# Post-norm two-layer block on one core: another assignment of two groups to the linear attention's buffers, four more early idle products, other priorities

## The chip, the cores and the metric

The kernel runs on one core of one Trainium2 chip. The metric is device time in microseconds (us) of one execution, lower is better. The time before is 608.35 us, the median of three runs (604.67 to 611.22). One further execution was profiled; it took 606.87 us, and its profile spans 605.1 us from the first instruction to the last.

Engine names in the profile: PE is TensorE (products; PEld its weight loads), DVE VectorE, ACT ScalarE, POOL GpSimd, SP the engine that issues the DMAs. L984 is line 984 of the kernel.

## The reference

Two layers, each an attention and a feed-forward part, with a layer norm behind each of the four residual sums. Shapes: x is 2 x 1024 x 128, all float32.

```python
x = layernorm(x + L0_attn(x))   # 8 heads, softmax over 1024 keys, 16-wide q/k, 128-wide v summed over heads
x = layernorm(x + L0_ffn(x))    # 128 -> 512 gated by silu, 512 -> 512 gelu, 512 -> 512 gelu, 512 -> 128
x = layernorm(x + L1_attn(x))   # linear attention, 4 heads of 32: short convolutions, delta rule in chunks of 32
x = layernorm(x + L1_ffn(x))    # +-1 weights: 256 -> 512 relu, 512 -> 512 relu, 512 -> 128
```

The delta rule is the part that the change touches:

```python
T = inv(eye + tril(kbeta k^T, -1)); u = T @ v; w = T @ kbeta     # per chunk of 32
for each of the chunks, in order:                                # a state S per batch and head
    u_i = u_i - w_i @ S
    o_i = q_i @ S + tril(q_i k_i^T) @ u_i
    S   = S + k_i^T @ u_i
o = gate * o + (1 - gate) * (p0 * v + p1 * fir_short(v) + p2 * fir_long(v))
o = rmsnorm(o) * rms_w @ Wo
```

## The kernel before, in words

**Tiling.** The 2048 rows of x are handled as four groups of 512: (0,0), (0,1), (1,0), (1,1), that is batch and half, called here the first to the fourth group. In the first attention there are eight units of 2 heads; two units make one group. A unit has two passes: `pass1` computes scores (L904) and takes their row maxima (L906 on DVE, for the first unit L909 and L912); a small transpose and two DMAs put the negated maxima back as an extra row of the queries (L921, L923, L925); `pass2` computes scores again (L944), exponentiates (L946 on ACT) and multiplies with the values (L951). The feed-forward part `ffn0` (L984) follows a group's attention, then `l1_attn`, then `ffn1` (L1502, L1503). Most wide products use a rounded part and a remainder of the activations, so that each weight is used with two products of 128x512.

**The linear attention** of one group goes through these steps: `l1prep` (transposes L802, convolutions as four products each, L1138), `l1gate` (L1187), `l1gram` (64 products of 32x32 tiles, L1087), `l1inv` (the triangular inverse, 30 small DVE operations at L1248 and L1249), `l1v` (values), `l1fir` (the long filter: 128 small products L1310, with Toeplitz blocks loaded by DMA into two small buffers `nm` and `pr`, or into a pool of five buffers of their own for the second and fourth group), `l1T`, `l1wu`, `l1scan` (16 dependent steps), `l1out`, `l1rms` (norm, product with Wo at L1494, layer norm). The group (1,1) needs the state of (1,0), and (0,1) that of (0,0).

It has two forms. The *early* form (`late` false) does the inverse first, and the filter after the scan; a scan step is four 32x32 products (L1087), the outputs are added in one accumulator (L1418, then L1474), and much of the elementwise work is on POOL. The *late* form does the filter ahead of the inverse; a scan step is one 128x128 product (L1451) with a block-diagonal operand that ACT has written before (`spread`, L1443: 16 copies a group), and elementwise work is on DVE and ACT.

**Buffers.** Three sets of buffers hold a linear attention at work: LA, allocated at the start, and two more, b and c, that take the place of the first attention's buffers when that has ended. `PLAN` says which set serves which groups in turn, `EARLY` for how many of a set's first jobs the early form is used. So before, LA serves the first group (early form) and later the fourth (late form), b the second and c the third.

**Order.** The program is recorded in full, then ordered by a planner in the kernel: a list scheduler with a price per instruction. An instruction's rank is its place in a backward plan minus 1000 times the entry of `AHEAD` for its step and group. `RUN` has two further settings: `switch`, a penalty in rank for changing the tile mode on PE, and `target`, the amount of recent PE work below which the planner puts an idle product (L1654, a product of constants that nobody reads) where it finds PE without work. So the order on each engine is fixed in the program, and the engines run it in order.

**Start.** PE begins with `KW` idle products on constants (L1555). Meanwhile SP loads x and the weights. Eleven weight blocks (`raw`, L726; two buffers) are rounded by ACT (L729), the remainder is taken by POOL (L731), and the pair goes back to DRAM (L732). x is normed, transposed (L802), copied by ACT (L831), and projected for the first unit (L681, evicted by ACT at L691 and L687 and by DVE at L692 and L688); the first group's other projections follow (L845, L846, L847).

Of the kernel before, what the change touches and what calls it, by code (L numbers as in the profile page):

```python
# [14 lines left out]
AX = mybir.AxisListType  # L15

MARK = HOOK = None
RUN = {'dummies': True, 'target': 3733.1600, 'rewarm': False, 'switch': 48514.8000}
TURNS = 5
AHEAD = {  # L20
    "ffn0": {"00": 114.739, "01": 79.0168, "10": 93.113, "11": 16.0},
    "ffn0b": {"00": 28.2844, "01": 46.0158, "10": 3.8711, "11": -177.442},
    "ffn0c": {"00": 7.2297, "01": 25.7048, "10": -2.4362, "11": -60.4919},
    "ffn1": {"00": -191.539, "01": -121.481, "10": -24.0187, "11": 13.6298},
    "ffn1b": {"00": -284.165, "01": -22.3296, "10": -26.57, "11": -37.1254},
    "ffn1c": {"00": -256.6, "01": -72.7131, "10": -43.7013, "11": -63.3199},
    "l1T": {"00": 58.5553, "01": 22.3564, "10": -115.222, "11": -15.058},
    "l1fir": {"00": 17.0418, "01": -65.313, "10": -9.4956, "11": -94.8684},
    "l1gate": {"00": 17.4596, "01": 74.4737, "10": -71.5563, "11": -51.9871},
    "l1gram": {"00": 71.0216, "01": 57.0343, "10": -34.4912, "11": -131.985},  # L30
    "l1inv": {"00": 101.529, "01": 187.238, "10": 97.6443, "11": -28.7276},
    "l1out": {"00": 8.2038, "01": 36.0016, "10": -49.0412, "11": -16.0023},
    "l1prep": {"00": 54.5467, "01": 18.6949, "10": -147.8, "11": -271.429},
    "l1rms": {"00": 19.507, "01": -139.242, "10": 56.2064, "11": -6.9188},
    "l1scan": {"00": 163.921, "01": -154.275, "10": -73.3537, "11": 123.217},
    "l1v": {"00": -45.706, "01": -14.4063, "10": -35.6576, "11": -265.782},
    "l1wu": {"00": 79.4419, "01": -19.5293, "10": -135.414, "11": -46.8271},
    "norm_in": {"0": 132.526, "1": 94.3253},
    "pass1": {"0": -45.1577, "1": -30.2813, "2": -37.2483, "3": 95.0868, "4": 22.2969, "5": -1.3221, "6": 36.2671, "7": 34.121},
    "pass2": {"0": -76.6421, "1": -27.8145, "2": 96.4425, "3": 23.5257, "4": 37.498, "5": 101.764, "6": 71.2041, "7": 34.7045},  # L40
    "post": {"00": 115.214, "01": 91.5204, "10": 25.9715, "11": 449.774},
    "prep": {"": 90.1269},
    "stacks": {"00": 12.9701, "01": -34.2909, "10": 54.0568, "11": 10.2821},
    "stk": {"0": -41.2247, "1": -35.7513, "2": 76.077, "3": 65.1726, "4": -27.8862, "5": 37.4738, "6": -56.9189, "7": 103.575},
    "warm": {"": 115.175},
    "weights": {"": 146.31},
}
HALVES, RU = 1, 1
KW = 40
ZLO, CVG, XH, TR, FE = 0, 1, 1, 5, 1  # L50
O1, O2, O3, O4 = 0, 1, 1, 1
LEND = (4, 2)
# [2 lines left out]
NI = 26  # L55
TB = 4
FA0 = 1
EARLY = {"fa": 2, "la": 1}
BANKS = (1, 2, 1, 1)
XJ = {"0": 3, "l": 1, "1": 3}  # L60
PLAN = [
    [("0", 0), ("0", 1), ("0", 2), ("0", 3), ("1", 0), ("1", 1), ("1", 2), ("1", 3)],
    [("l", 0), ("l", 3)],
    [("l", 1)],
    [("l", 2)],
]
GROUPS = [(0, 0), (0, 1), (1, 0), (1, 1)]

# [466 lines left out]
def body(ctx: ExitStack, tc: tile.TileContext, A, out, dbg=None):  # L535
# [6 lines left out]
    def mark(label):  # L542
        plan.marks.append((len(nc.cur_bb.bb.instructions), label))
        if MARK:
            MARK(nc, label)
# [1003 lines left out]
    def front():  # L1549
# [3 lines left out]
        wp = psv.tile([128, 512], F32, tag="pv", name="wp")  # L1553
        for n in range(KW):
            nc.tensor.matmul(wp, rest[:, 0:128], rest, start=True, stop=True)  # L1555
# [45 lines left out]
    def jobs(bufs, todo, extra=None):  # L1601
        for n, (kind, gi) in enumerate(todo):
# [3 lines left out]
            while need not in ready or (kind == "l" and GROUPS[gi][1] and ("l", GROUPS.index((GROUPS[gi][0], 0))) not in ready):  # L1606
                yield None
            yield from {"0": ffn0, "l": l1_attn, "1": ffn1}[kind](bufs, gi, n >= EARLY.get(bufs.nm, 0))
            if kind in "0l":
# [36 lines left out]

    plan.run(rank, least=WARM, **RUN)
    mark("idle")
# [109 lines left out]
```

## Time and profile before

| what | value |
|---|---|
| median of three runs | 608.35 us (604.67 to 611.22) |
| profiled execution | 606.87 us, of it 605.1 us span |
| mean granted TensorE clock | 0.988 |
| products of the first attention's last unit end (L951) | 355.6 us into the span |
| last product of the whole program (L1066) | 597.4 us |
| exponentials, L946 on ACT | 131.4 us and 12.1 us, 603 and 605 ns each |
| row maxima, L906 on DVE | 141.2 us, 681 ns each |
| loads of ACT's function tables | 17, 1283 ns each |

The shares of busy time are means over stages. From about 45 us to about 560 us PE is busy nearly all the time; ahead of that it shares the lead with loads and evictions, and behind it a chain of dependent steps sets the end. Two things are to be kept in mind for PE. A float32 product shows as two matmul records and two weight loads (64 products at L1474 show as 128 records), a rounded or bfloat16 one as one of each. And a stretch marked "issue" is one in which PE waited for nothing that the profile shows.

### The profile page before, as it was taken

How to read it: one execution, taken by the hardware profiler on the slowest of the kernel's cores; microseconds unless marked ns; L12 is line 12 of the kernel's file. 1: busy time of each engine (PE TensorE's matmuls, PEld its weight loads, DVE VectorE, ACT ScalarE, POOL GpSimd, SP SyncE). 2: the span in 40 equal slices, each digit the busy share in tenths (PEclk: the TensorE clock that was granted, in tenths of full speed). 3: DMA queues.
4: the chain of work that ended last, by engine and by line, in shares of the span. 5: the costliest groups of instructions: out<-in, count | busy, mean ns of one | idle time of the engine just before them, and what ended most of it. 6: DMA issues, size and time to landing. Idle time of an engine off the chain costs nothing.

```text
span 605.1 us, 17727 instructions
## 1 busy us (share of the span) xinstructions
PE 568.6 (94%) x7496; PEld 360.5 (60%) x7496; DVE 402.2 (66%) x975; ACT 340.5 (56%) x619; POOL 232.2 (38%) x317
## 2 busy tenths in 40 slices
PE   8789999999999999999999999999999998899984
PEld 4255455557675656556656466756777576677753
DVE  4758787786645798488974212397654967777763
ACT  3656467765768776865858564444434543434331
POOL 8845017212300726030397024437562361623210
PEclk9979999999999999999999999999989999999998
DMA  8886330025221306203121045315343013102220
GB/s 280 295 296 220 77 87 2 2 53 163 98 71 70 86 14 180 70 1 106 54 73 43 31 144 181 105 28 170 110 158 121 4 38 101 40 22 78 98 72 17
DMA packets 26737, 58.39 MB, mean 96 GB/s; under 512 B 4065, under 2 KB 12897, under 8 KB 26658
## 3 DMA queue, kind: packets, MB, share of 16 engines
q1 hardware_dynamic: 26658, 57.26, 30.2%
q8 instruction: 59, 0.97, 0.7%
q14 instruction: 20, 0.16, 0.1%
HBM read 41.19 MB, written 8.39 MB: 82 GB/s over the span
## 4 chain that ended last, share of the span: by engine, by line
PE 78%; DMA 7%; ACT 5%; DVE 4%; issue 2%; POOL 2%; SPq 1%; POOLq 0%; DVEq 0%; ACTq 0%
PE ps L984 19%; PE pv L951 10%; PE s L944 10%; PE ps L904 9%; PE ps L1087 7%; PE ps L1138 5%; PE ps L1503 4%; PE ps L1502 4%; DMA raw<-wf 2%; PE ps L1451 2%; PE ps L1310 2%; DMA x<-x 1%; DMA q<-mr 1%; DMA nm<-toep 1%; ACT p L946 1%
## 5 line engine op out<-in xcount | busy, mean ns | idle before, releaser
L906 DVE TENSOR_REDUCE mp<-ps 128x1 f32<-128x512 f32 x224 | 141.2, 681 | 52.0 <-PE ps L904 51.3
L946 ACT ACTIVATE p<-s 128x512 f32<-128x512 f32 x236 | 131.4, 603 | 49.4 <-PE s L944 40.8
L984 PE MATMUL ps<-ahi,w 128*128 128x512 f32 x352 | 123.1, 420 | 1.2 <-ACT u L1038 0.8
L944 PE MATMUL s<-q,k 128*128 128x512 f32 x236 | 92.1, 423 | 2.5 <-DMA q<-mr 1.6
L904 PE MATMUL ps<-k,q 128*128 128x512 f32 x240 | 85.2, 419 | 2.7 <-DVE m L912 1.4
L984 PEld LDWEIGHTS ps<-ahi,w 128*128 128x128 f32 x352 | 64.5, 190 | 28.4 <-issue 6.1
L951 PE MATMUL pv<-p,va 128*32 128x512 f32 x512 | 72.6, 601 | 0.0
L984 PE MATMUL ps<-alo,w 128*128 128x512 f32 x176 | 70.0, 400 | 0.2 <-POOL alo L998 0.2
L944 PEld LDWEIGHTS s<-q,k 128*128 128x128 f32 x236 | 42.3, 188 | 33.3 <-ACT p L946 16.8
L904 PEld LDWEIGHTS ps<-k,q 128*128 128x128 f32 x240 | 43.9, 190 | 26.5 <-DVE mp L906 10.2
L1502 PE MATMUL ps<-ahi,w 128*128 128x512 f32 x96 | 40.6, 423 | 3.2 <-DVE alo L1518 2.3
L1503 PE MATMUL ps<-alo,w 128*128 128x512 f32 x96 | 39.4, 412 | 1.1 <-DVE alo L1518 0.7
L1517 ACT ACTIVATE ahi<-ps 128x512 fp32r<-128x512 f32 x32 | 18.5, 597 | 37.5 <-PE ps L1503 37.4
L984 PEld LDWEIGHTS ps<-alo,w 128*128 128x128 f32 x176 | 33.5, 190 | 8.8 <-issue 0.7
L1138 PE MATMUL ps<-xT,wc 128*128 128x512 f32 x72 | 35.9, 609 | 0.8 <-POOL xT L1125 0.8
L1020 POOL TENSOR_TENSOR alo<-u,ahi 128x512 fp32r<-128x512 f32 x16 | 20.5, 1282 | 38.9 <-ACT ahi L1019 38.8
L1518 DVE SCALAR_TENSOR_TENSOR alo<-ps,ahi 128x512 fp32r<-128x512 f32 x32 | 21.4, 685 | 13.5 <-ACT ahi L1517 13.2
L786 POOL TENSOR_SCALAR r<-mv 128x4 f32<-128x4 f32 (+1 forms) x24 | 6.3, 265 | 60.9 <-DVE mv L784 55.5
L951 PEld LDWEIGHTS pv<-p,va 128*32 128x32 f32 x512 | 13.1, 108 | 26.6 <-issue 24.6
L1038 ACT ACTIVATE u<-ps,small 128x512 f32<-128x512 f32 x16 | 11.0, 687 | 26.9 <-PE ps L984 26.7
L976 POOL TENSOR_TENSOR y<-y,x 128x256 f32<-128x256 f32 x8 | 6.3, 788 | 51.4 <-DVE y L975 51.4
L1454 DVE TENSOR_TENSOR tt<-ps,an 128x32 f32<-128x32 f32 x64 | 11.9, 186 | 20.9 <-PE ps L1087 12.5
(274 smaller groups left out, 1034.9 us busy)
## 6 DMA issues: line engine op xcount, KB each, us to landing
w<-wd SPq DMA_DIRECT2D x56, 512.0 KB
wd<-w SPq DMA_DIRECT2D x14, 512.0 KB
raw<-wf SPq DMA_DIRECT2D x11, 256.0 KB
pj<-vC SPq DMA_DIRECT2D x32, 64.0 KB
toep<-toep SPq DMA_DIRECT2D x16, 128.0 KB
q<-hi SPq DMA_DIRECT2D x14, 128.0 KB
k<-hi SPq DMA_DIRECT2D x28, 64.0 KB
xt<-x SPq DMA_DIRECT2D x4, 256.0 KB
```

The lines of the kernel that those rows point to most:

```text
L904: nc.tensor.matmul(p, q[:, s * 128:(s + 1) * 128], d, start=True, stop=True)
L906: nc.vector.tensor_reduce(mp[:, s, e, i:i + 1], p, AX.X, ALU.max)
L944: nc.tensor.matmul(s2, ks[e][:, t * 128:(t + 1) * 128], q[:, i * 512:(i + 1) * 512], start=True, stop=True)
L946: nc.scalar.activation(p, s2, AF.Exp, scale=0.25)
L951: together([nc.tensor.matmul(pv[32 * j:32 * j + 32, :], va[:, t - 1, 2 * pr + j % 2, :], pend[j % len(pend)], start=(t == 1), stop=(t == 8 ...
L984: nc.tensor.matmul(p, w(k), a(k), start=(k == 0 and n == 0), stop=(k == nk - 1 and n == len(pr) - 1))
L1020: nc.gpsimd.tensor_tensor(lo[:, m, :], u, hi[:, m, :].bitcast(F32), ALU.subtract)
L1087: r.append(nc.tensor.matmul(p(hs), lhsT(hs), rhs(hs), start=True, stop=True, tile_position=(32 * h, 32 * h)))
L1138: nc.tensor.matmul(p, wc[:, w, t, :], xTh[:, t:t + 512], start=t == 0, stop=t == 3)
L1502: nc.tensor.matmul(p, w(k), ahi(k), start=(k == 0), stop=False)
L1503: nc.tensor.matmul(p, w(k), alo(k), start=False, stop=(k == nk - 1))
L1518: nc.vector.scalar_tensor_tensor(lo, p, 0.0, hi.bitcast(F32), ALU.max, ALU.subtract)
```

## The change

Three settings are changed, and the priorities with them; no function is edited.

```diff
-RUN = {'dummies': True, 'target': 3733.1600, 'rewarm': False, 'switch': 48514.8000}
+RUN = {'dummies': True, 'target': 4397.5100, 'rewarm': False, 'switch': 72754.5000}
...
-    "l1out": {"00": 8.2038, "01": 36.0016, "10": -49.0412, "11": -16.0023},
-    "l1prep": {"00": 54.5467, "01": 18.6949, "10": -147.8, "11": -271.429},
+    "l1out": {"00": 43.059, "01": 90.2521, "10": -47.2495, "11": 1.5469},
+    "l1prep": {"00": 44.7584, "01": -7.3587, "10": -133.55, "11": -298.276},
...
-    "weights": {"": 146.31},
+    "weights": {"": 109.692},
 }
...
-KW = 40
+KW = 44
...
-EARLY = {"fa": 2, "la": 1}
+EARLY = {"fa": 2, "la": 2}
...
 PLAN = [
     [("0", 0), ("0", 1), ("0", 2), ("0", 3), ("1", 0), ("1", 1), ("1", 2), ("1", 3)],
-    [("l", 0), ("l", 3)],
+    [("l", 0), ("l", 2)],
     [("l", 1)],
-    [("l", 2)],
+    [("l", 3)],
 ]
```

All 27 rows of `AHEAD` have other numbers. LA now serves the first and the third group, both in the early form, and the set c the fourth group, in the late form.

Counted in the two built programs, instructions that differ in number (from -> to):

| engine | instructions |
|---|---|
| PE | L1451 48 -> 32; L1474 64 -> 128; L1555 40 -> 44; L1654 35 -> 47 (in all 4470 -> 4534 products) |
| ACT | L1443 48 -> 32; L1259 12 -> 8; L1329 3 -> 2; table loads 17 -> 19 (one more at L946, one more at L1038) |
| DVE | L1334 6 -> 4; L796 on attention outputs 12 -> 8; L1288, L1344, L1347, L1430 3 -> 2 each |
| POOL | L1261 4 -> 8; L796 on attention outputs 20 -> 24; L1337 and L1338 2 -> 4 each; L1288, L1331, L1344, L1347 1 -> 2 each; L1368 6 -> 4; L1431 3 -> 2 |
| SP | 251, the same DMAs in another order |

The order changes on all engines. The main moves on PE, by place among the products (0 is the first; first to last product of a step):

| step, group | before | after |
|---|---|---|
| idle products L1555 | 37 ahead of the first transposes, 3 behind | 44 ahead |
| last unit's `pass2` ends | 1719 of 4470 | 1703 of 4534 |
| `l1rms` first group | 2291-2294 | 2138-2141 |
| `l1prep` third group | 2136-2295 | 2143-2318 |
| `l1scan` second group | 3013-3555 | 2922-3267 |
| `l1scan` third group | 3557-4024 | 3212-3467 |
| `l1fir` third group | 2559-2871 | 3432-3773 |
| `l1prep` fourth group | 2769-3015 | 3162-3272 |
| `l1gram`, `l1T` fourth group | 3087-3198, 3632-3863 | 3343-3423, 3829-4006 |
| `l1wu`, `l1scan` fourth group | 3869-4148, 4155-4287 | 4011-4220, 4235-4349 |

On ACT, the third rounding L729 moves from behind the two copies L831 to ahead of them, and each later one stands one to four evictions further ahead than before.

## Prediction

> **What bounds the kernel now.** I read the page first, then busy time by stretches, the groups by line, the chain of waits, and the timeline of the start.
>
> ```profile
> PE 568.6 (94%) x7496; PEld 360.5 (60%) x7496; DVE 402.2 (66%) x975; ACT 340.5 (56%) x619; POOL 232.2 (38%) x317
> PEclk9979999999999999999999999999989999999998
> ```
>
> PE leads at 94%, and its clock is low in one slice only. Stretches (us; busy us and instructions of PE, PEld, DVE, ACT, POOL; clock; DMA):
>
> ```profile
> 40.00:44.00 4.00, 4.00 (x14) 3.02 (x14) 1.40 (x4) 2.50 (x5) 2.44 (x3) 0.50 1.03 371
> 475.00:495.00 20.00, 19.77 (x656) 13.48 (x659) 16.27 (x43) 10.85 (x24) 13.63 (x18) 1.00 0.09 29
> 495.00:515.00 20.00, 17.03 (x684) 13.75 (x674) 14.76 (x53) 8.03 (x21) 2.17 (x5) 1.00 0.28 78
> 515.00:535.00 20.00, 18.34 (x677) 13.88 (x677) 16.07 (x51) 7.03 (x19) 12.95 (x13) 1.00 0.09 30
> 583.00:605.00 22.00, 12.52 (x53) 8.75 (x52) 9.56 (x29) 5.12 (x9) 2.53 (x4) 0.90 0.08 25
> ```
>
> PE has 1 to 3 us of slack per 20 us late on, and a tail of dependent steps. Groups (count | busy us, mean ns | idle before):
>
> ```profile
> L1451 PE MATMUL ps<-tt,pj 128*128 128x32 f32 x96 | 17.1, 260 | 0.3 <-DVE tt L1454 0.3
> L1654 PE MATMUL ip<-rest 128*128 128x512 bf16 x35 | 9.9, 381 | 0.0
> L1474 PE MATMUL ps<-tt,kv 32*32 32x32 f32 x128 | 1.5, 194 | 0.0
> ```
>
> Chain of waits (start, us, what):
>
> ```profile
> 151.00 2.73 PE ps L984 x12
> ...
> 360.60 4.37 DMA nm<-toep
> ...
> 501.89 1.42 PE ps L1087 x84
> 503.31 0.34 PE ps L1451 x2
> ...
> 505.33 0.84 issue
> 506.17 0.92 PE ps L1418 x60
> ...
> 512.65 0.94 issue
> 513.60 0.94 PE ps L1087 x62
> ```
>
> From these rows I price PE's work as it follows back to back: a wide product 0.2275 us (2.73/12), a small L1087 product 0.032 (about two records of 0.016), a scan step L1451 0.356 (17.1/48), an idle product 0.22 (four took 0.88 in the chain), a float32 512-column product 0.86 (L1138: two records took 0.86), a filter product 0.024, a transpose 0.13. The control: between the fourth group's first product (463.4 us) and the last product of its `l1wu` (543.7), 1380 products at these prices are 79.8 us; the trace has 80.3. The prices carry; what they miss is the sum of waits.
>
> The start, on ACT:
>
> ```profile
> 13.32 1.07 ACT L831 COPY xhT<-ps 128x512 f32<-128x512 f32 x2 [2.78 <-PE ps L802]
> 17.65 0.62 ACT L729 CAST w<-raw 128x512 fp32r<-128x512 f32 x1 [3.25 <-DMA raw<-wf]
> 18.18 0.68 ACT L691 ACTIVATE q<-ps,bqk 96x512 fp32r<-96x512 f32 x1
> ```
>
> The first eviction L691 stands behind a weight block that lands at 17.65.
>
> **The change, part by part.** *Start.* Seven more idle products ahead of the transposes put them 7 x 0.27 = 1.9 us later; covered, because the third L729 now stands ahead of the copies L831. The bytes ahead of its block on SP's queue are the same, so the copies wait for 17.65 and end at 19.35. L691 then also waits for the fourth block, at 20.89 before, now behind one 512 KB write in place of two, about 1.5 us earlier: L691 at about 20.3, 2.1 us late. Each further block needs POOL's L731 two blocks before (0.62 + 1.28 us, then about 3 us of load), so L846 comes at about 29.0 (26.91 before). Then it shrinks: before, the fifth L909 waited for the eighth block at 32.80; now that block stands four evictions earlier and ahead of the 448 KB load of `ku`, which puts the fifth L909 at 33.4 (33.33 before). The ninth block then delays the next three by 2 us, the small copy L923 (37.37 before) by 1.3, `biasv` (41.23) by 0.4. L944 starts at 45.57 and PE is full from 48 us on: what is late there stays late. I take +0.8; bounds -1.0 (the 1.4 us of idle PE in 32 to 36 us refilled) and +2.5 (nothing recovered).
>
> In the rows, the clock was 0.65 in 36 to 40 us and 0.50 in 40 to 44, though after the first 3 us no idle time of PE ahead of it was over 1.2 us; a thin stretch was enough. So I keep the same loss, and the new gap of about 3.3 us before L681 (15.7 to 19.0) at most doubles eight products of 0.6 us, inside waits. [...]
>
> *PE's work.* 16 scan steps go, -5.7; 64 products at L1474 come, 64 x 0.023 = +1.5; 12 idle products, 12 x 0.22 = +2.6: -1.6. But PE also pauses at "issue": nine times between 497.4 and 528.1, every 3.8 us, 0.08 to 0.94 us each, in stretches of 32 to 35 products' records and as many loads per us. In instructions the change adds 64 x 4 + 12 x 2 - 16 x 4 = 216; at some 256 per 3.8 us that is +3.2 where small products stand close. The new ones of the third group stand partly there. Bounds -4.2 (idle products free) and +3.2; I take -1.0, near the busy rows. [...]
>
> *ACT.* 16 copies L1443 go (-4.7 us, off PE's path); two table loads come, 2 x 1.28, in the last unit's exponentials (one more alternation of gelu and exp). PE lost 0.65 us in 350 to 360 with two alternations. Bounds 0 and 2.6; I take +0.6. DVE loses ten instructions (some 6 us), POOL gains 13 (some 12 us, 38% busy now) in the third group's filter and inverse, whose result is wanted hundreds of products later: nothing, as long as the third group is not last.
>
> *Shared LA.* The third group's `l1prep` must follow the first group's `l1rms`. Its Wo product waits for the chain L1478 to L1491, which at the row's durations (0.7, 0.7, 0.6, 0.7, POOL 0.2 and 2.9, 0.7, 0.7 and handovers) needs 8.8 us; PE has 9.5 us of work between the two. Bounds 0 and 2; +0.3. Queued behind that wait on PE is everything.
>
> *Fourth group.* Its chain now starts at product 3162 and has 63.1 us of PE work to the end of `l1wu`, against 79.8. From the last `l1gram` product to the first `l1T` PE has 22.4 us (25.1 before; the trace took 25.8). In between lie 52 DVE operations, 20 us, four ACT operations of 0.6 and handovers: about 24. From `l1T` to `l1wu` 9.1 us of work are enough (the second group did it in 9.3). So PE waits about 2 us. Bounds 0 and 9 (below).
>
> *Scan and tail.* 16.4 us of work lie in the last scan, 18.9 before (17.7 in the trace); a step of 0.36 plus L1454 0.19 and two handovers is 0.85 at least (first group: 0.85), 13.6 in all. I take -1.0; bounds -2.5 and 0. What follows, 34.4 us, is the same chain.
>
> Sum: 0.8 - 1.0 + 0.6 + 0.3 + 2.0 - 1.0 = +1.7 on 606.87, 608.6. The median of the runs lies 1.5 above that execution; between 608.6 and 610.1 I put 609.0.
>
> **The rivals.** *Slower: the fourth group's chain binds.* If `l1prep`-`l1gram`, `l1gram`-`l1T` and `l1wu`-`l1scan` keep the times that they had (20.6, 25.8, 15.2) where PE now has 17.9, 22.4 and 11.8 us of work, PE waits 2.7 + 3.4 + 3.4 = 9.5 us: 609.0 - 2.0 + 9.5 = 616.5. It decides from about 6 us of wait. For it: the compressed start; against: in the trace those times equal PE's own work, so the chain may be shorter.
>
> *Faster: the late pauses go.* The fourth group's stretch holds 4048 PE instructions in place of 5354 and 19 idle products as before; if the pauses (4.5 us in 497 to 528) and 2.5 us of idle in 495 to 535 fall away there, and the idle products fall only into waits (-2.6), 609.0 - 9.6 = 599.4. Against it: 5336 instructions in place of 3694 now stand between the attention's end and that point, and bring pauses of their own.
>
> *The changed order does nothing where it counts*: PE's work by the prices is equal to within 2 us, so only start and tables count, +1.4: 609.8 with the median's offset. It is inside the forecast's size class.
>
> **How the numbers follow.** Forecast (with the third rival) 0.44, slower rival 0.30, faster rival 0.26. A change of 1%, 6 us, is about what a measurement of this kernel can tell from none. The range reaches to both rivals' values: 599.4 to 617. The chances of faster, same and slower are these three.
>
> **What would show it.** In the changed profile: ACT's third L729 at about 17.6 with L831 behind it, L846 near 29; L944 starting by 46; the fourth group's first transpose near 480, and "issue" pauses more frequent ahead of it; idle on PE ahead of its `l1T` of 1 to 3 us (over 5: the slower rival; none, and few pauses: the faster); L1451 32 products. I am wrong on the whole if the last unit's L951 ends more than 5 us from 359.

## The result, and the profile after

The changed kernel takes 614.75 us (median of 16 runs, 610.18 to 618.74), the kernel before 608.72 in the runs beside them (16 runs, 604.67 to 612.90): ratio 1.011, 95% interval 1.0086 to 1.0135. It is slower by about 1%. Ratios, and the means in the table of the experiments, leave out runs over 1.5% above the fastest of the same kernel; medians hold all runs. The profiled execution took 612.65 us, 610.9 of it span, 5.8 more than before.

The busy line and the granted clock of the page:

```profile
PE 573.1 (94%) x7608; PEld 361.8 (59%) x7608; DVE 396.3 (65%) x965; ACT 335.3 (55%) x600; POOL 243.3 (40%) x330
PEclk9879999999999999999999999899999999899998
```

Two slices of the start are low now in place of one, and two behind the attention (not counting the last). Stretches (us; busy us and instructions of PE, PEld, DVE, ACT, POOL; clock; DMA share, GB/s):

```profile
20.00:24.00 4.00, 4.00 (x6) 1.45 (x7) 2.48 (x3) 2.00 (x4) 4.00 (x4) 0.57 0.81 228
40.00:44.00 4.00, 4.00 (x10) 2.46 (x11) 1.40 (x4) 2.61 (x6) 3.38 (x4) 0.50 0.83 253
44.00:48.00 4.00, 4.00 (x20) 3.64 (x19) 2.14 (x6) 1.19 (x2) 3.91 (x4) 0.58 0.59 237
392.00:396.00 4.00, 3.79 (x79) 2.90 (x79) 2.70 (x8) 0.59 (x1) 1.49 (x2) 0.57 0.01 4
475.00:495.00 20.00, 18.96 (x421) 11.86 (x410) 9.81 (x32) 7.60 (x18) 1.79 (x6) 1.00 0.01 3
495.00:515.00 20.00, 19.00 (x609) 12.17 (x605) 13.09 (x36) 5.51 (x10) 10.71 (x18) 1.00 0.15 48
515.00:535.00 20.00, 17.45 (x639) 12.14 (x632) 15.48 (x53) 4.66 (x8) 5.73 (x6) 0.91 0.35 101
583.00:605.00 22.00, 16.90 (x72) 11.04 (x71) 12.39 (x39) 6.74 (x11) 2.53 (x4) 1.00 0.11 36
```

Two of these stretches before:

```profile
20.00:24.00 4.00, 2.95 (x7) 0.78 (x6) 2.99 (x5) 2.88 (x5) 3.44 (x5) 1.00 0.75 205
44.00:48.00 4.00, 3.76 (x21) 2.73 (x20) 3.09 (x9) 2.59 (x6) 4.00 (x4) 0.99 0.27 105
```

Read the clock column. Taken in steps of 1 us it is 1.00, or falls to 0.50 in stretches of about 3.4 us, each of which loses 1.7 us of full clock. The profile of before has them at 37-44 (two, one behind the other) and at 446-451, that of after at 20-24, 37-48 (three), 392-396, 470-474 and 525-529: seven in place of three. (Each has some 2 us more at its very end, where PE has nothing left to do.)

Against this the milestones of the two profiles are: first L944 45.6 and 48.8 us, last L951 355.6 in both, end 605.1 and 610.9. So the start costs 3.2 us, the attention behind it is 3.2 us shorter, and the part behind the attention is 5.7 us longer.

The start on ACT, with what ended the idle time in brackets:

```profile
17.35 0.62 ACT L729 CAST w<-raw 128x512 fp32r<-128x512 f32 x1 [7.00 <-DMA raw<-wf]
17.88 1.07 ACT L831 COPY xhT<-ps 128x512 f32<-128x512 f32 x2
19.89 0.68 ACT L691 ACTIVATE q<-ps,bqk 96x512 fp32r<-96x512 f32 x1
21.98 0.58 ACT L687 CAST d<-ps 96x512 fp32r<-96x512 f32 x1 [1.41 <-PE ps L681]
29.73 1.31 ACT L846 ACTIVATE hi<-ps,bqk 128x512 fp32r<-128x512 f32 x2
```

The copies L831 stand behind a weight block, as the order says; PE idles 2.69 us ahead of the first L681, at 18.51, and then runs at half clock (0.50 in 21 to 23), so that L687 waits 1.41 us for PE.

A pause late in the program, on PE:

```profile
389.38 0.98 PE L1087 MATMUL ps<-kq 32*32 32x64 f32 x55
392.21 0.47 PE L1087 MATMUL ps<-kq 32*32 32x64 f32 x9 [1.86 <-issue]
```

It waited for nothing that the profile shows, in the middle of a row of small products, and the stretch right behind it (392:396 above) ran at 0.57.

### The profile page after: what moved, and what is told of

Its sections match the earlier page's. It is cut to its first block, busy times and chain, and to the rows that moved or that the text cites. A ratio compares the mean times of both kernels' runs of the same rounds, so it can differ in the third digit from the quotient of the medians.

```text
span 610.9 us, 17941 instructions
## 1 busy us (share of the span) xinstructions
PE 573.1 (94%) x7608; PEld 361.8 (59%) x7608; DVE 396.3 (65%) x965; ACT 335.3 (55%) x600; POOL 243.3 (40%) x330
## 4 chain that ended last, share of the span: by engine, by line
PE 80%; DVE 6%; DMA 5%; ACT 4%; issue 2%; SPq 2%; POOL 1%; POOLq 0%; DVEq 0%; ACTq 0%
PE ps L984 21%; PE pv L951 10%; PE s L944 10%; PE ps L904 9%; PE ps L1087 8%; PE ps L1138 5%; PE ps L1503 3%; PE ps L1502 3%; DMA raw<-wf 3%; DVE mp L906 2%; PE ip L1654 1%; PE ps L1310 1%; PE ps L802 1%; PE ps L1451 1%; PE ps L845 1%
## 5 line engine op out<-in xcount | busy, mean ns | idle before, releaser
L946 ACT ACTIVATE p<-s 128x512 f32<-128x512 f32 x236 | 131.7, 603 | 39.1 <-PE s L944 27.7
L944 PE MATMUL s<-q,k 128*128 128x512 f32 x236 | 91.4, 420 | 0.0
L904 PE MATMUL ps<-k,q 128*128 128x512 f32 x240 | 87.7, 424 | 3.4 <-DVE m L912 1.4
L984 PEld LDWEIGHTS ps<-ahi,w 128*128 128x128 f32 x352 | 63.2, 188 | 26.7 <-issue 4.3
L951 PE MATMUL pv<-p,va 128*32 128x512 f32 x512 | 71.2, 601 | 0.0
L984 PE MATMUL ps<-alo,w 128*128 128x512 f32 x176 | 70.8, 405 | 0.0
L904 PEld LDWEIGHTS ps<-k,q 128*128 128x128 f32 x240 | 44.3, 191 | 31.2 <-DVE mp L906 12.8
L944 PEld LDWEIGHTS s<-q,k 128*128 128x128 f32 x236 | 42.5, 188 | 27.1 <-ACT p L946 14.6
L1503 PE MATMUL ps<-alo,w 128*128 128x512 f32 x96 | 40.4, 421 | 1.1 <-DVE alo L1518 0.7
L951 PEld LDWEIGHTS pv<-p,va 128*32 128x32 f32 x512 | 13.3, 108 | 26.9 <-issue 24.6
L879 POOL MEMSET q<- 2x1024 f32 x5 | 4.7, 949 | 59.9 <-PE s L944 56.0
L1042 ACT ACTIVATE z<-ps,small 128x512 f32<-128x512 f32 x16 | 11.0, 689 | 26.1 <-PE ps L984 25.8
```

Source lines behind the costliest of these rows:

```text
L904: nc.tensor.matmul(p, q[:, s * 128:(s + 1) * 128], d, start=True, stop=True)
L944: nc.tensor.matmul(s2, ks[e][:, t * 128:(t + 1) * 128], q[:, i * 512:(i + 1) * 512], start=True, stop=True)
L946: nc.scalar.activation(p, s2, AF.Exp, scale=0.25)
L951: together([nc.tensor.matmul(pv[32 * j:32 * j + 32, :], va[:, t - 1, 2 * pr + j % 2, :], pend[j % len(pend)], start=(t == 1), stop=(t == 8 ...
L984: nc.tensor.matmul(p, w(k), a(k), start=(k == 0 and n == 0), stop=(k == nk - 1 and n == len(pr) - 1))
L1503: nc.tensor.matmul(p, w(k), alo(k), start=False, stop=(k == nk - 1))
```

## The experiments

In the table, "lost" is (1 - mean granted clock) x span, and "rest" is the time less that, means over a kernel's runs. A ratio is to runs of before on the same chip, while "lost" and "rest" of before differ by up to 2 us among the chips (last row). e1 to e4, e5 to e8, and e9 with e10 ran on one chip each, with runs of before beside them. The changed kernel's own row stands first.

| kernel | median us | ratio to before, 95% | clock | lost us | rest us |
|---|---|---|---|---|---|
| changed | 614.75 | 1.0110 (1.0086-1.0135) | 0.978 | 13.6 | 601.0 |
| e1 changed, old start | 611.72 | 1.0049 (1.0004-1.0094) | 0.983 | 10.1 | 601.4 |
| e2 before, new start | 613.66 | 1.0106 (1.0060-1.0153) | 0.979 | 12.8 | 601.4 |
| e3 changed, late moves | 615.71 | 1.0128 (1.0078-1.0178) | 0.978 | 13.6 | 602.1 |
| e4 e1 and e3 together | 612.44 | 1.0053 (1.0017-1.0090) | 0.984 | 9.9 | 601.4 |
| e5 before, start filled | 606.52 | 0.9954 (0.9912-0.9996) | 0.988 | 7.0 | 598.8 |
| e6 e1, start filled | 604.88 | 0.9965 (0.9933-0.9997) | 0.991 | 5.4 | 599.6 |
| e7 changed, no late idle products | 619.90 | 1.0193 (1.0149-1.0237) | 0.956 | 27.1 | 592.4 |
| e8 sharing alone | 631.21 | 1.0387 (1.0339-1.0435) | 0.967 | 20.7 | 610.6 |
| e9 changed, one L729 back | 616.01 | 1.0071 (1.0035-1.0108) | 0.978 | 13.4 | 602.4 |
| e10 changed, own start filled | 613.02 | 1.0025 (0.9984-1.0067) | 0.988 | 7.4 | 605.5 |
| before: e1-e4 / e5-e8 / e9-e10 | 609.21 / 607.75 / 611.16 | 1 | 0.986 / 0.985 / 0.983 | 8.4 / 9.3 / 10.3 | 600.1 / 598.5 / 600.9 |

Within the runs of one kernel the same holds: over 18, 19 and 21 runs of before the time rises by 0.87, 0.75 and 0.80 us for each us of lost clock (correlation 0.85, 0.72, 0.91); over the 16 of the changed kernel by 0.58 (0.80).

**e1 and e2: the start changes sides.** The planner's lists of each engine are rewritten behind its run; a table gives the start's instructions by step and number.

```diff
+    START = {
...
+        "Activation": "norm_in:0/0-1 weights/11 weights/0-1 norm_in:0/2-3 weights/2 stk:0/0-1 weights/3 stk:0/2-3 weights/4 stk:0/4-6 weights/5 stk:0/7 stacks:00/0-1 weights/6 pass1:0/0-3 weights/7 pass1:0/4-7 weights/8 pass1:0/8-10 weights/9 prep/0 pass1:0/11-12 weights/10 pass1:0/13 pass2:0/0 pass1:0/14-15 pass2:0/1 pass1:0/16 pass2:0/2-4 pass1:0/17",
...
+        plan.order[e] = [next(want) if o in have else o for o in L]
     order = plan.order["PE"]
```

> The changed kernel with the first instructions of every engine (PE 117, DVE 64, ACT 50, POOL 60, SP 55, to about 50 us) in the order of the kernel before; the four new idle products stay, at the very front. Nothing behind is moved. Theory A (the granted clock): the loss is time at half clock, in stretches of about 3.4 us that cost 1.7 us each; the profile of the changed kernel has them at 20-24, 37-48 (three in a row), 392-396, 470-474 and 525-529, that of before at 37-44 (two) and 446-451. The start's order makes the one at 20-24 and one of 37-48: without it the first pass2 starts at 45.6 in place of 48.8, the mean clock rises by 0.005, and the kernel ends about 3.3 us earlier, ratio to before 1.005 to 1.006. Theory B (the fourth group's chain sets the end): PE gets its work earlier, but the end does not move by more than 1 us, ratio 1.010 to 1.011.

> The kernel before with the first instructions of every engine in the order of the changed kernel (40 idle products, all ahead of the transposes); nothing else. Theory A: half clock at 20-24 and a third stretch in 37-48, first pass2 at 48.8, ratio 1.005 to 1.006, mean clock lower by 0.005. Theory B: the start is swallowed later, as the profiles seem to say where the last unit of the attention ends at 357.1 in both: ratio 0.999 to 1.002.

Measured 1.0049 and 1.0106. With the old start the changed kernel comes down by 0.6% (1.0110 to 1.0049, some 3.7 us), its lost clock by 3.5 us; with the new start the kernel before goes up by 1.06% (0.60 to 1.53), its lost clock by 4.4. Theory B falls: the start is not swallowed. The second figure is above what theory A gave, with 1.3 us more in the rest. e2 has 40 early idle products, all at the front, so the four new ones aren't needed for the loss. In e1's profile the stretches are not those that theory A expected: the one at 20-24 is gone, but another stands at 23-27, and the first L944 comes at 47.6, not 45.6. (e4, with the same start, has it at 44.2.)

**e3 and e4: the late waits.** In the chain of waits of the changed kernel a Toeplitz block stands, issued behind loads of the fourth group's values:

```profile
522.04 3.24 DMA nm<-toep
...
525.32 0.63 PE ps L1310 x32
525.95 0.72 PE ps L1503
526.67 0.43 PE ps L1502
```

Behind it a wide product takes 0.43 us in place of 0.23, at half clock (0.50 in 526 to 528).

```diff
+    L = plan.order["PE"]
+    L[1876:1885] = L[1880:1885] + L[1876:1880]
+    L = plan.order["SP"]
+    L[231:235] = [L[233], L[234], L[231], L[232]]
     order = plan.order["PE"]
```

> The changed kernel with two moves late in the order: on SP, the last two Toeplitz loads of the third group stand ahead of one load of the fourth group's values and one of weights; on PE, five wide products of ffn1b stand ahead of the fourth group's first filter products. Theory A: PE's waits of 0.50 us (values) and 1.25 us (Toeplitz block) at 522 to 525 go, and with them the half clock at 525-529; the fourth group's l1T starts at about 529 (the inverse ends at 528.2) in place of 532.0, the end comes 2 to 3.4 us earlier, ratio 1.006 to 1.008. Theory B: the inverse is late next, l1T still starts at 529 at the earliest, and behind it the dependent scan steps set the end: 0 to 1.5 us, ratio 1.0085 to 1.011. If the half clock does not come from those waits, it stays and only up to 1.7 us are gained.

> Both edits of the two other kernels together: the changed kernel with the start's order of before and with the two late moves. Theory A: the gains add, 5 to 6.8 us, ratio 0.999 to 1.003, and only the stretches at half clock at 37-44, 392-396 and 470-474 are left (mean clock about 0.985). Theory B: at most 1.5 us, ratio 1.008 or more.

Measured 1.0128 and, with the old start, 1.0053: no gain (e4 equals e1), and neither figure is in a range that was expected. Both DMA waits are gone from the profile of e3, and in their place stands, on PE:

```profile
525.36 0.25 PE L1310 MATMUL ps<-pj,toep 64*32 64x16 f32 x6
527.48 0.99 PE L1310 MATMUL ps<-pj,toep 64*32 64x16 f32 x90 [1.86 <-issue]
```

and half clock at 528-533 (0.50 in 529 to 532); the fourth group's `l1T` starts at 531.2 in place of 532.0. PE came earlier to a place where it paused at "issue", and waited there instead. So the gain that theory A expected falls, and the sum expected of e4 with it. Whether the DMA waits made the half clock of the changed kernel is not settled by this: a pause as long took their place, and half clock followed it too.

**e5, e6 and e10: idle products in the thin stretches of the start.** `KW` is raised, all other instructions keep their order, and the new L1555 stand where PE waits.

```diff
-KW = 40
+KW = 59
```

The kernel of this diff is e5; e6 has `KW = 63` on the kernel of e1, e10 `KW = 73` on the changed kernel with its own start.

> The kernel before with 19 more idle products L1555, put where PE waits at the start (2 and 3 ahead of the first two L681 pairs, 4 ahead of the third xhT pair, 1, 1, 4 and 4 among the first L904); all engines otherwise in the order of before. Theory A (the granted clock; in the runs so far the time less (1 - mean clock) x span is 600 to 602 us for every kernel): PE thinly used between 15 and 37 us is what brings half clock there; filled, one to two of the stretches of 1.7 us go, mean clock up by 0.003 to 0.006, ratio 0.994 to 0.997. Theory B (loads and evictions set the start): the clock may rise, but PE waits for the same evictions, ratio 0.999 to 1.002; if the idle products stand in the way, up to 19 x 0.22 = 4.2 us more, 1.007.

> The changed kernel with the start in the order of before and the same 19 idle products in its waits. Theory A: the gain of the start's order (0.6% in the kernel that has it alone) and that of the filling add, ratio 0.999 to 1.002, lost clock down from 11.0 to about 8 us. Theory B: as without the filling, 1.005.

> The changed kernel with its own order everywhere and 29 more idle products L1555 in the waits of its start (12 ahead of the first L681, where PE waits 2.7 us; 1, 4, 2, 1, 5 and 4 further on). If the start costs by the clock alone, the third rounding may stay where it is: lost clock 5 to 7 us, ratio 0.996 to 1.000, as with the old start filled. If it costs by late evictions as well, the ratio stays 0.3 to 0.5% above that, 1.000 to 1.003. If idle products at half clock stand in the way, 1.005 or more.

Measured 0.9954, as theory A had it; 0.9965, better than its 0.999; and 1.0025. The page of e6:

```profile
PE 570.1 (95%) x7627; PEld 357.8 (59%) x7627; DVE 397.2 (66%) x965; ACT 335.3 (56%) x600; POOL 242.5 (40%) x330
PEclk9999999999999999999999999999998999999998
```

and the stretch in which before stood at 0.50, in the profile of e5:

```profile
40.00:44.00 4.00, 3.26 (x20) 2.28 (x20) 2.23 (x7) 2.26 (x5) 2.05 (x3) 1.00 1.00 370
```

Twenty products in place of fourteen pass in these 4 us. Products that nobody reads made both kernels faster, before by 0.5%, the changed one by 0.8% against e1. With the start of before, and filled, the two orders differ by 0.1%, less than the intervals tell apart (e5 and e6, on one chip). Filling the changed kernel's own start brings it from 1.0110 to 1.0025, but it helps the start of before as much: filled, the new start is 0.6% above the old one (e10, e6), as it is unfilled (changed, e1). The lost clock of e10 is down to 7.4 us, its rest is 4.6 us above that of before. Whether late evictions or the 29 products in the way (ten more than in e6) make that rest is open. The profile doesn't decide it: L944 starts at 52.0 there, but half clock stands at 28-32 and 45-52, in spite of the filling (clock 0.982, the mean of the runs is 0.988). e5 and e6 beat both kernels; their intervals end 0.04% and 0.03% below before.

**e7: the late idle products out.**

```diff
+    plan.order["PE"] = [o for o in plan.order["PE"] if o != FULL]
     order = plan.order["PE"]
```

> The changed kernel without its 47 late idle products L1654, every other instruction in the same order. Theory A: they hold the clock in the stretches of small products, where PE pauses at issue; without them there are two or more further stretches at half clock, ratio 1.012 to 1.020 and mean clock lower by 0.004 or more. Rival (they are work that stands in the way, 47 x 0.22 = 10.3 us, and the twelve new ones are part of the loss): ratio 0.995 to 1.008 and the same clock.

Measured 1.0193 and a clock of 0.956: theory A. Against the changed kernel its rest falls by 8.6 us (0.18 for each of the 47; the chips differ, which is worth up to 2 us), and 13.5 us of clock are lost for it. Its page has the fall in the last third:

```profile
PEclk9879999999999999999999999998989999789867
```

**e8: the sharing alone.**

```diff
-EARLY = {"fa": 2, "la": 1}
+EARLY = {"fa": 2, "la": 2}
...
-    [("l", 0), ("l", 3)],
+    [("l", 0), ("l", 2)],
```

> The kernel before with PLAN and EARLY of the change alone: 40 early idle products and the priorities of before. The start keeps the order of before; behind it the planner puts the instructions anew. If the exchange of the buffers makes the loss behind the attention, ratio 1.004 to 1.010 with it alone. If it is the priorities that make it, 0.998 to 1.002; but priorities that were not found for these buffers can cost by themselves, then 1.01 to 1.03 and nothing follows for the parts.

Measured 1.0387, the case from which nothing follows for the parts: with the old priorities the last scan step ends at 588.8 us in its profile, at 569.1 in the changed kernel.

**e9: one rounding back.**

```diff
+    L = plan.order["Activation"]
+    L.insert(7, L.pop(5))
     order = plan.order["PE"]
```

> The changed kernel with one move: the third rounding L729 stands behind the two copies L831 on ACT again, as in before; all else as changed. If this one place makes the gap ahead of the first L681 and with it the half clock at 20-24 (theory A), the first L681 is back at about 16 us, the mean lost clock falls from 13.6 to 11 to 12 us and the ratio is 1.004 to 1.007, as with the whole start of before. If the later roundings, which also stand further ahead, make it, 1.009 to 1.011.

Measured 1.0071 (1.0035 to 1.0108), and a lost clock of 13.4, as without the move. The time alone decides nothing, since both cases lie in the interval. The clock speaks against the one place, but weakly, since before itself lost 8.4 us on one chip and 10.3 on this one. The first L681 is back at 15.56, but now PE idles 3.71 us ahead of the fourth, at 22.28, and half clock at 23-27 and 40-48 follows. That the other roundings, also further ahead, moved the gap on is likely, but wasn't tried.

## Why the prediction was right and wrong

The time lies in the range, between the likeliest case and the slower rival, and the likeliest case (within 1%) did not come. That the range holds is partly luck: its upper part stood for waits for the inverse, which did not come, and what came in their place, more half clock, had no term. By steps:

**Start, +0.8 (bounds -1.0 to +2.5): the step that failed.** The order of events came nearly as worked out (forecast in brackets): third L729 at 17.35 (17.65), L691 at 19.89 (20.3), L846 at 29.73 (29.0), the fifth L909 at 33.9 (33.4). Even the doubling of eight products after the new gap is there (20:24 at 0.57). What failed is "So I keep the same loss". The doubled products made L687 wait for PE and the evictions later, L923 came at 40.86 (38.7 by the prediction), and half clock in 37 to 48 took three stretches, not two. L944 started at 48.8, not by 46. In time the start is worth 3.7 us (e1) to 6.5 (e2, 3.6 to 9.3), where the upper bound was 2.5. That the start's order costs this is shown: e2 differs from before in nothing else, and loses 4.4 us of clock and 1.3 of rest; e1 gets 3.5 us of clock back and nothing of the rest. That it costs by the clock alone is not shown: with less clock lost than before has on that chip (e10, 7.4 against 10.3 us), the new start is still 0.6% above the old one (e6).

In the two profiles a stretch at half clock lasts 3.4 us, or two or three times that where they stand one behind the other, and the 16 runs of the changed kernel have clocks from 0.966 to 0.985. The length of one pause doesn't decide by itself whether a stretch comes: in the changed kernel the pause of 1.86 us at 390.35 has one behind it (0.57 in 392 to 396), at the same place in e7 a pause of 2.31 us has none (1.00 in 392 to 396).

**PE's work, -1.0.** The groups after are as counted:

```profile
L1654 PE MATMUL ip<-rest 128*128 128x512 bf16 x47 | 14.9, 393 | 0.0
L1451 PE MATMUL ps<-tt,pj 128*128 128x32 f32 x64 | 11.5, 262 | 0.7 <-DVE tt L1454 0.5 <-ACT ahi L1517 0.2
```

But the price of a scan step, 0.356 from busy time over count, was too high. In the chain of the changed kernel:

```profile
492.53 0.34 PE ps L1451 x2
492.87 0.32 PE ps L1503
493.18 0.19 PE ps L1087 x8
493.38 0.43 PE ps L1502
```

A wide product behind small ones takes 0.43 there, at a clock of 1.00; with a step between, step and wide product take 0.34 + 0.32. The step adds 0.23, so by this estimate 16 of them gave 3.7 us, not 5.7, and the sum of the three kinds is +0.4, not -1.6, before any pause. The control agreed because it was made on a stretch with 32 steps, too dear, and 52 wide products, too cheap among small ones: PE idled 5.8 us within its 80.3, so the priced 79.8 left next to no room for waits that were there. On the fourth group's stretch after, with 8 steps and 63 wide products, the prices gave 63.1 us, and the trace has 70.2 (481.3 to 551.5), 4.8 of it idle and 1.7 lost to half clock. The pauses at "issue" sum to 7.5 us before and 7.7 after: the bound of +3.2 for them was not needed.

**Tables, +0.6, and shared buffers, +0.3.** A loss by the tables isn't seen, though no run has them alone: from the first L944 to the last L951 the changed kernel is 3.2 us faster. That gain goes with the order: the eight profiles with the changed order take 306.6 to 307.2 us there, the three with that of before 309.6 to 310.0. It was not forecast, and its cause wasn't tried. The shared buffers cost about what was forecast: ahead of the third group's first transposes (L802 at 403.92) PE waits 0.57 us for L1071, which takes up the first group's Wo product.

**Fourth group's chain, +2.0.** It starts at 481.3 (480 forecast), and from the last `l1gram` to the first `l1T` PE takes 27.4 us against 22.4 of work: 5.0 in place of 2.0, within the bounds, 3.5 of it idle and 1.7 half clock. The cause was another one than forecast: the inverse ended at 528.2, and PE came to `l1T` at 532.0, held up by its own pauses, two DMA waits (0.50 and 1.25 us) of the third and fourth groups' filters, whose loads queue on SP (a queue that the prediction did not follow), and half clock. The slower rival gave 616.5, nearest to the time, but by waits for the inverse; e3 removed the two DMA waits, a pause of 1.86 us took their place, and the end stayed.

**Scan and tail, -1.0.** From the last `l1wu` to the end 61.4 us became 59.4: -2.0, within its bounds.

**The faster rival** is out: the pauses did not go.

What stays open is the rest of the loss behind the start: e1 is 0.49% above before (0.04 to 0.94), while with both starts filled (e6, e5) the difference is 0.1%. In single profiles the part behind the attention goes with the number of half-clock stretches in it: in the changed order 251.2 us with one (e6), 254.2 and 255.0 with two (e3, e10), 255.3 and 258.7 with three (changed, e9), 258.1 and 260.2 with four (e1, e4); in the order of before 248.5 with none (e5), 249.5 and 252.9 with one (before, e2). Whether the changed order meets them more often, or these few executions did, is not settled, and what brings a stretch at one pause and none at another wasn't tried. The parts of the change behind the start, buffers and priorities, weren't told apart either (e8).

## What to carry to other kernels

Where PE is the bound, sum up the granted clock in steps of a microsecond before pricing anything else: here four more stretches at half clock, 1.7 us each, outweighed every term of the sum. A thin stretch at the start can be worth filling with products that nobody reads, also when the engine waits for loads there anyway: here 19 of them took 0.5% off the kernel before (e5) and 0.8% off e1 (e6). And price a product by what it adds between its neighbours (here an estimated 0.23 us for a scan step), not by busy time over count (0.356); a control on one mix of products (79.8 priced, 80.3 measured) proves little for another (63.1 and 70.2).

## What the runs showed that was not expected

Pauses at "issue" came at nearly fixed numbers of instructions in rows of small products, whichever products these were: counting matmul records from the start, before and after both pause at records 4009, 4263 and 4518 (1.34, 0.53, 0.30 us before; 0.68, 1.76, 0.37 after), e3 and e6 at the same three, 254 and 255 records apart; in the row of before from 497.98 to 517.05 us six pauses of 0.29 to 0.94 us stand 126 to 128 records apart. Not every such place has one (e1 has none at 4009, e5 none at 4263), and in e8 the row is shifted (4523 and 4777). When the waits of 0.50 and 1.25 us ahead of such a place were taken away (e3, record 6302), a pause of 1.86 us took their time. And one order of instructions does not have one clock: e1 and e4 have the same order up to 515 us, and their profiles show half clock at 23-27 and 40-48 in the one and at 35-43 in the other.
